# Layer 0's weight products with seven block products instead of eight, the last six batches' norm summed by TensorE, and another order of the preamble

## The chip, the core and the metric

The kernel runs on one NeuronCore of a Trainium2 chip: TensorE (matrix products, PE in the profile), VectorE (DVE), ScalarE (ACT), GpSimd (POOL), SyncE (SP, which here only issues DMAs), an SBUF and a PSUM of eight banks of 128 x 512 fp32. The metric is the device time of one execution in microseconds, the median of the runs. All arithmetic is fp32.

## The reference, cut to what matters

The input `x` is (64, 256, 128): 64 batches, 256 graph nodes, 128 channels. `adj` is 256 x 256. Four layers follow one another; each adds its result to its input and normalises over the channels.

```python
def ln(x): return (x - mean(x)) / sqrt(var(x) + 1e-5)          # over the 128 channels

# layer 0: powers of adj, seven weights (the second adjacency is the same adj)
x = ln(x + x@W0 + (A x)@(W1+W4) + (A A x)@(W2+W5) + (A A A x)@(W3+W6))
x = ln(x + A (x @ w) + bias)                                    # layer 1
x = ln(x + (D A^ D x) @ W.T + b)                                # layer 2
h = x                                                           # layer 3: 5 gated steps
for _ in range(5):
    m = A h                                                     # m_in = m_out
    z = sigmoid(m @ w3.T + h @ u3.T + b3);  r = sigmoid(m @ w4.T + h @ u3.T + b4)
    hv = tanh(m @ w5.T + (r * h) @ u5.T + b5)
    h = (1 - z) * h + z * hv
out = ln(x + h)
```

## The kernel before, in words

**Groups.** The 64 batches are worked in 32 groups of two batches (`NB = 2`), named by their first batch: 0, 2, ... 62. A group's tile is 128 partitions by 512 columns: 2 batches x 2 node halves (`T = 2`) x 128 channels. Up to ten groups are under way at once (`ACTIVE = 10`), in different layers, so that one group's products run while another waits for its elementwise work.

**Order.** Nothing is left to a run-time scheduler. `Plan` collects every operation with an engine, a cost, a lag and a rank, and `Plan.order` lays them out by a list schedule; each engine then executes its instructions strictly in that order. The buffers are slots by kind: `bank` (8, PSUM), `w` (64 tiles of 128 x 512), `th`, `q` and small ones for statistics. `Group.rank` sets which group goes first among ready operations. `pre` adds the operations of the preamble (weights, adjacency and constants), with a rank of their own; `fetch` and `load` are its DMAs, on the queue of SP or GpSimd. `Group.pe`, `dve` and `act` add a group's operations.

**A product.** `mm(o, lhsT, rhs, start, stop)` (L199) is one TensorE product, `lhsT` stationary (128 x 128), `rhs` moving (128, 256 or 512 wide). In the trace an fp32 product leaves two MATMUL records, a transpose through `ident` one.

**The adjacency products** (`propagate`, `seven`) already use seven block products instead of eight for a 2 x 2 block product, with sums ahead on GpSimd (L599, L603, L606) and sums behind on VectorE and ScalarE (L627 to L649).

**Layer 0.** With `q = A A x` it computes `s0 = x@W_0 + q@W_2 + A (x@W_1 + q@W_3)`, where the `W_k` in `w0s` are the summed weights, with the identity for the residual in `W_0` and each row's mean taken off, so that the result is centred. For each node half `t`, a bank `py0t` takes both products at once, 256 columns of weights wide:

```python
mm(o, (tiles if near else pairs)(xT)[:, b, t], w01.ap[:, 0:2, :], b == 0, True, shared=True)
mm(o, tiles(qT)[:, b, t], w0s.ap[:, 2:4, :], False, True, shared=True)
```

So a group has 2 halves x 2 batches x 2 = 8 products 256 wide. ScalarE copies the half that belongs under `A` to `v` (`moved`, L756), TensorE adds `A v` onto the other half (`second`, L764, 256 wide), ScalarE copies the sum to `s0` (`summed`, L768). The first two groups (`HEAD = 4` batches, `near`) get `xT` by TensorE transposes (L659). The other 30 get it by a VectorE transpose of 32 x 32 blocks (L730, `tx`), a store to DRAM (L733) and two loads (L738). For these the contraction rows come out permuted, and `w0p` is a copy of `w0s`'s first two weights with rows permuted alike (`permuted`, four DMAs, L308).

**Norms.** Layers 0 to 2 have centred sums: `spread_of` squares on ScalarE with an accumulated sum (L513), GpSimd takes the power -1/2 (L517, L518), ScalarE scales (L529). The last norm is not centred. It has `bn_stats` and `bn_aggr` on VectorE (L487, L491), the power on GpSimd (L498), and a scale and shift on ScalarE (L549).

**Layer 3** holds `hT`, the transposed state. Each step has five products 512 wide (`pr`, `ph`), two sigmoids and a tanh on ScalarE (L707), and `rh`, `d`, `e` and the new `hT` on VectorE (L714).

**The end.** After the last step the state must be turned back. Most groups do it by a VectorE transpose and DRAM (`tn`, `hn`). The last two groups (`END = 4` batches: 60 and 62) have TensorE transpose `hT` (L659, `pth`), VectorE add `y` (L541), take statistics and normalise too (L554).

**The preamble.** The first products need `ident` (GpSimd), the adjacency `a_nat`, its transpose `aT` and square `a2T`, the raw weights `w0_raw` of layer 0 and the first `x`. `warmed` issues 14 transposes that only keep TensorE busy (`WARM`). The small weights of layers 1 to 3 come by SP and GpSimd DMAs, are summed (`both`), centred (`wb`) and transposed (`transposed`, L397), all at ranks between 0.1 and 0.4.

Of the kernel before, what the change touches and what calls it, by code (L numbers as in the profile page):

```python
# [13 lines left out]
P = 128  # L14
# [5 lines left out]
END = 4  # L20
STEPS = 5
WARM = 14
# [135 lines left out]
def kernel(  # L158
# [42 lines left out]
    SHAPES = {"bank": [P, 512], "x": [P, 512], "w": [P, 512], "th": [P, 384], "q": [P, P], "st": [P, Q * 6], "mv": [P, Q * 2],  # L201
              "ve": [P, Q], "rs": [P, Q]}
    slots = {"bank": BANKS, "x": ACTIVE + 3, "w": 64, "th": 10, "q": 10, "dram1": 8, "dram2": 16, "st": 12, "mv": 12, "ve": 24, "rs": 12}
# [11 lines left out]
    def pre(rank, engine, cost, run, reads=(), writes=(), lag=None, joint=False):  # L215
        lag = lag or {"SP": 2300, "PE": 260, "DVE": 260, "ACT": 130, "POOL": 100}[engine]
        plan.add(engine, cost, lag, rank, run, reads, writes, joint=joint)
# [4 lines left out]
    def fetch(rank, o, src, v, queue):  # L222
        e, cost = QUEUES[queue]
        pre(rank, queue, cost, lambda: e.dma_start(o, src), [], [v], lag=3000, joint=True)
# [57 lines left out]
    w0_raw = load(0.01, "w0_raw", [P, C, K0], w0)  # L282
# [21 lines left out]
    w0p = constant("w0p", [P, 2, C])  # L304

    def permuted():
        for r in range(4):
            nc.sync.dma_start(w0p.ap.rearrange("(j r) k c -> r j k c", r=4)[r], w0s.ap[32 * r:32 * (r + 1), 0:2, :])  # L308

    pre(1.2, "SP", 1800, permuted, [w0s], [w0p])  # L310
# [61 lines left out]
    fetch(0.1, wb.ap[:, 0, :], w1, wb, "SP")  # L372
    for i, b in ((1, b1), (2, b2)):
        fetch(0.1, wb.ap[:, i, :], bass.AP(tensor=b.tensor, offset=b.offset, ap=[[0, P], [1, C]]), wb, "POOL")
    pre(0.35, "DVE", 1100, lambda: centre(wb, wbm), [wb], [wb, wbm])
    w1c, b1c, b2c = ((wb, wb.ap[:, i, :]) for i in range(3))
    raw = {name: load(0.1, f"raw_{name}", [P, src.shape[1]], src, False, "SP")
# [11 lines left out]
    def transposed(name, *parts_):  # L389
        ps, v = temp(f"p_{name}"), constant(name, [P, len(parts_) * P])  # L390

        def run():
            for i, src in enumerate(parts_):
                if src is raw["w2"]:
                    mm(ps.ap[:, i * P:(i + 1) * P], src.ap, less.ap, True, True)
                else:
                    nc.tensor.transpose(ps.ap[:, i * P:(i + 1) * P], src.ap, ident)  # L397

        n = len(parts_) * P
        pre(0.4, "PE", len(parts_) * 110, run, [*parts_, less], [ps])  # L400
        pre(0.4, "ACT", act_cost(n), lambda: nc.scalar.copy(v.ap, ps.ap[:, :n]), [ps], [v])
        return [(v, v.ap[:, i * P:(i + 1) * P]) for i in range(len(parts_))]
# [6 lines left out]
    for i, src in enumerate((w3_b, w4_b, w5_b, u3_b, u3_b, u5_b)):  # L409
        fetch(0.2, braw.ap[:, i:i + 1], src.rearrange("(p o) -> p o", o=1), braw, "POOL")  # L410
# [27 lines left out]
    class Group:  # L438
# [5 lines left out]

        def view(self, ap):
            return ap[self.start:self.start + self.nb].rearrange("b (t p) c -> p (b t) c", p=P)
# [11 lines left out]
        def add(self, engine, cost, lag, run, reads=(), writes=(), joint=False, behind=()):  # L458
            after = behind if self.first else self.gate
            self.count += 1  # L460
            op = plan.add(engine, cost, lag, self.rank(), run, reads, writes, after, joint)
            self.first = self.first or op
            self.last = op
            return op
# [15 lines left out]
        def statistics(self, tag, s, near):  # L480
            st, mv, ve, rs, nm = (self.val(k, n + tag) for k, n in (
                ("st", "st"), ("mv", "mv"), ("ve", "ve"), ("rs", "rs"), ("ve", "nm")))
            kept = () if near else (nm,)

            def stats():
                for q in range(self.q):
                    nc.vector.bn_stats(st.ap[:, q * 6:(q + 1) * 6], nat(s)[:, q, :])  # L487

            def aggr():
                for q in range(self.q):  # L490
                    nc.vector.bn_aggr(mv.ap[:, 2 * q:2 * q + 2], st.ap[:, q * 6:(q + 1) * 6])  # L491
                mean, var = (mv.ap.rearrange("p (q k) -> p k q", k=2)[:, k] for k in range(2))
                nc.vector.tensor_scalar(ve.ap, var, EPS, None, op0=OP.add)
                if not near:
                    nc.vector.tensor_scalar(nm.ap, mean, -1.0, None, op0=OP.mult)

            def scales():
                nc.gpsimd.tensor_tensor(rs.ap, ve.ap, half[:, :self.q], op=OP.pow)  # L498
                if not near:
                    nc.gpsimd.tensor_tensor(mv.ap[:, :self.q], nm.ap, rs.ap, op=OP.mult)  # L500

            self.dve(stats, [s], [st], 195 * self.q)
            self.dve(aggr, [st], [mv, ve, *kept], 67 * self.q + (142 if near else 240))
            self.add("POOL", 1010 if near else 1300, 100, scales, [ve, *kept], [rs] if near else [rs, mv])
            return mv, rs
# [33 lines left out]
        def residual(self, tag, ps, resid, left=lambda v: v.ap, right=lambda v: v.ap):  # L539
            s = self.val("w", "s" + tag)  # L540
            self.dve(lambda: nc.vector.tensor_add(right(s), left(ps), right(resid)), [ps, resid], [s])  # L541
            return (s, *self.statistics(tag, s, self.start >= B - END))

        def normalise(self, tag, s, mv, rs):
# [7 lines left out]
            def near():  # L552
                for q in range(self.q):
                    nc.vector.tensor_scalar(nat(y)[:, q, :], nat(s)[:, q, :], mv.ap[:, 2 * q:2 * q + 1],  # L554
                                            rs.ap[:, q:q + 1], op0=OP.subtract, op1=OP.mult)

            if self.start >= B - END:
                self.dve(near, [s, mv, rs], [y], 257 * self.q)
            else:
                self.act(run, [s, mv, rs], [y], 390 * self.q)  # L560
            return y
# [155 lines left out]
        def record(self):  # L717
# [5 lines left out]
            if near:  # L723
                xT, w01 = self.copied("xT", self.transposes("x", x_)), w0s
            else:

                w01 = w0p
                turn, far = self.val("w", "tx"), self.val("dram", "dx")
                xT = self.val("w", "xT")
                self.dve(lambda: nc.vector.transpose(  # L730
                    turn.ap.rearrange("p (r b i t) -> p r b t i", r=4, t=T, i=32),
                    x_.ap.rearrange("p (b t r j) -> p r b t j", r=4, t=T, j=32)), [x_], [turn])
# [9 lines left out]
            v, s0 = self.val("w", "v"), self.val("w", "s0")  # L742
            py = []

            for t in range(T):
                p = self.val("bank", f"py0{t}")
                py.append(p)

                def first(p=p, t=t):
                    for b in range(self.nb):  # L750
                        o = p.ap[:, b * 2 * C:(b + 1) * 2 * C]
                        mm(o, (tiles if near else pairs)(xT)[:, b, t], w01.ap[:, 0:2, :], b == 0, True, shared=True)
                        mm(o, tiles(qT)[:, b, t], w0s.ap[:, 2:4, :], False, True, shared=True)

                def moved(p=p, t=t):
                    nc.scalar.copy(parts(v)[:, t], four(p)[:, :, 1, :])  # L756

                self.pe(pe_cost(2 * C, 2 * self.nb), first, [xT, qT, w01, w0s], [p])
                self.act(moved, [p], [v], 55 + 107 * self.nb)
            for t in range(T):  # L760

                def second(p=py[t], t=t):
                    for kt in range(T):
                        mm(four(p)[:, :, 0, :], aT.ap[:, kt, t * P:(t + 1) * P], parts(v)[:, kt],  # L764
                           False, True, shared=True)

                def summed(p=py[t], t=t):
                    nc.scalar.copy(nat(s0).rearrange("p (b t) c -> p t b c", t=T)[:, t],  # L768
                                          four(p)[:, :, 0, :])

                self.pe(pe_cost(self.nb * C, T), second, [v, aT], [py[t]])
                self.act(summed, [py[t]], [s0], 55 + 107 * self.nb)
# [25 lines left out]
            for s in range(STEPS):  # L798
# [4 lines left out]
                r = self.gate_(f"r{s}", pr, AF.Sigmoid, rb)  # L803
                rh = self.tensor(f"rh{s}", OP.mult, r, hT)
# [7 lines left out]
                d = self.tensor(f"d{s}", OP.subtract, hv, hT)  # L812
                e = self.tensor(f"e{s}", OP.mult, z, d, into=pr)
# [8 lines left out]
            else:  # L822
                hT = self.tensor("hT", OP.add, hT, e, lambda v: v.ap.rearrange("p (k q i) -> p q k i", k=4, q=self.q),
                                 lambda v: v.ap.rearrange("p (q k i) -> p q k i", k=4, q=self.q))
                last = self.residual("3", self.transposes("h", hT), y)
# [68 lines left out]
```

## Time and profile before

| what | value |
|---|---|
| median of 3 runs | 1357.69 us (1357.1 to 1357.96) |
| the profiled execution | 1357.43 us |
| its span, first to last instruction | 1355.7 us |
| mean granted TensorE clock | 0.996 |
| TensorE busy, records of matmul | 1331.2 us, 6509 |
| VectorE / ScalarE / GpSimd busy | 953.2 / 756.0 / 678.0 us |
| first start of a TensorE record / last | 2.5 / 1345.8 us |
| layer 0's products, first and last start | 16.2 and 1080.9 us |

A row of the groups, for example `L199 PE MATMUL py<-v,aT 128*128 128x256 f32 x256`, names line, engine, operation, the tile written and the tiles read, the shape, and the number of records; a timeline row starts with its start in us and its length. A bracket at a row's end gives the engine's idle time ahead of it and what ended it. A matmul's length includes the drain of its pipeline, which overlaps the next one, so for TensorE the distance from start to start is the better price.

### The profile page before, as it was taken

Reading aid. Unit: us, or ns where it says so; the run is one execution under the profiler, and the core shown is the slowest. Engines: PE = TensorE matmul, PEld = TensorE weight load, DVE = VectorE, ACT = ScalarE, POOL = GpSimd, SP = SyncE. Lnnn points to the kernel's source line nnn. Section 1 sums busy time; section 2 is a strip of 40 time slices with the busy share of each in tenths; the row PEclk is TensorE's granted clock in tenths of the full one; section 3 lists DMA queues with packets and bytes.
Section 4 is the critical chain, followed back from the end, with each engine's and each line's share of the span. In section 5 each row is a group of like instructions: output and inputs, shape, how many; then the busy total and the mean of one; then the engine's idle time right before and its main releaser. Section 6 shows DMA issues by size and latency. Waiting matters only on the chain.

```text
span 1355.7 us, 21892 instructions
## 1 busy us (share of the span) xinstructions
PE 1331.2 (98%) x6509; PEld 922.0 (68%) x6509; DVE 953.2 (70%) x2343; ACT 756.0 (56%) x2398; POOL 678.0 (50%) x1095
## 2 busy tenths in 40 slices
PE   8999999999999999999999999999999999999995
PEld 7986666667676676776676667766776776566552
DVE  5366678778667677677767767776565778777778
ACT  4665464665456565657455466554655676444444
POOL 5786343654446544546364455543744685233322
PEclk9999999999999999999999999999999999999998
DMA  6322333434333322434243333332432233333333
GB/s 173 102 63 71 94 95 113 134 104 124 92 97 94 109 80 81 121 109 125 63 125 110 101 102 110 103 99 65 117 94 63 71 102 117 94 101 94 94 92 103
DMA packets 270214, 135.47 MB, mean 100 GB/s; under 512 B 175856, under 2 KB 241648, under 8 KB 270096
## 3 DMA queue, kind: packets, MB, share of 16 engines
q1 hardware_dynamic: 269840, 133.95, 34.1%
q8 instruction: 52, 0.85, 0.3%
q14 instruction: 66, 0.54, 0.1%
q0 software_dynamic: 256, 0.13, 0.1%
HBM read 67.57 MB, written 66.06 MB: 99 GB/s over the span
## 4 chain that ended last, share of the span: by engine, by line
PE 94%; DVE 3%; DMA 1%; issue 0%; ACT 0%; SPq 0%; POOL 0%; POOLq 0%; DVEq 0%; ACTq 0%
PE pr L199 30%; PE ph L199 20%; PE pmg L199 18%; PE py L199 15%; PE pm L199 7%; PE pmq L199 3%; DMA x<-in_x_dram 1%; DMA w_raw<-in_L_gnn_weight_dram 1%; DVE st L487 0%; DMA dx<-tx 0%; DVE s L541 0%; DVE rh L714 0%; DVE tx L730 0%; ACT y L529 0%; DVE y L554 0%
## 5 line engine op out<-in xcount | busy, mean ns | idle before, releaser
L199 PE MATMUL pr<-mg,w435u5T 128*128 128x512 f32 x640 | 320.3, 593 | 0.8 <-ACT r L707 0.8
L599 POOL TENSOR_TENSOR tsg<-h 128x256 f32<-128x256 f32 x128 | 96.4, 753 | 211.5 <-DMA h<-dh 145.0
L707 ACT ACTIVATE r<-pr,bsum 128x512 f32<-128x512 f32 x160 | 109.7, 686 | 151.1 <-PE pr L199 150.1
L714 DVE TENSOR_TENSOR rh<-r,hT 128x512 f32<-128x512 f32 x160 | 125.5, 787 | 71.6 <-ACT r L707 67.5
L707 ACT ACTIVATE pr<-pr,bsum 128x512 f32<-128x512 f32 x160 | 105.6, 660 | 120.7 <-PE pr L199 115.9
L199 PE MATMUL ph<-rh,w435u5T 128*128 128x512 f32 x320 | 164.1, 596 | 0.8 <-DVE rh L714 0.7
L714 DVE TENSOR_TENSOR d<-ph,hT 128x512 f32<-128x512 f32 x160 | 109.8, 686 | 78.3 <-ACT ph L707 77.3
L199 PE MATMUL ph<-mg,w435u5T 128*128 128x512 f32 x320 | 163.4, 593 | 0.0
L199 PE MATMUL pr<-hT,w2u3T 128*128 128x512 f32 x320 | 162.2, 592 | 0.0
L199 PEld LDWEIGHTS pr<-mg,w435u5T 128*128 128x128 f32 x640 | 109.0, 191 | 64.8 <-issue 48.6
L707 ACT ACTIVATE ph<-ph,bsum 128x512 f32<-128x512 f32 x160 | 105.5, 659 | 63.7 <-PE ph L199 62.9
L529 ACT ACTIVATE y<-s,rs 128x128 f32<-128x128 f32 x384 | 122.1, 392 | 15.4 <-POOL rs L518 14.7
L517 POOL TENSOR_SCALAR ve<-ve 128x4 f32<-128x4 f32 x96 | 22.6, 235 | 214.3 <-ACT y L513 214.2
L199 PEld LDWEIGHTS pmg<-s_aTp,tsg 128*128 128x128 f32 x768 | 102.1, 191 | 34.6 <-issue 30.7
L513 ACT ACTIVATE y<-s 128x128 f32<-128x128 f32 x384 | 113.7, 301 | 18.4 <-DVE s L536 18.2
L199 PEld LDWEIGHTS pmg<-aTp,h 128*128 128x128 f32 x512 | 88.0, 197 | 46.7 <-issue 35.1
L714 DVE TENSOR_TENSOR pr<-pr,d 128x512 f32<-128x512 f32 x160 | 110.6, 692 | 1.5
L627 DVE TENSOR_TENSOR usg<-usg,pmg 128x128 f32<-128x128 f32 x160 | 45.2, 284 | 91.9 <-PE pmg L199 67.2
L714 DVE TENSOR_TENSOR hT<-hT,pr 128x512 f32<-128x512 f32 x160 | 108.6, 680 | 1.7
L199 PE MATMUL pmg<-s_aTp,tsg 128*128 128x128 f32 x768 | 106.4, 275 | 0.0
L518 POOL TENSOR_TENSOR rs<-ve,half 128x4 f32<-128x4 f32 x96 | 99.6, 1038 | 8.0
L637 DVE TENSOR_TENSOR mg<-pmg,usg 128x256 f32<-128x256 f32 x160 | 67.1, 420 | 51.7 <-PE pmg L199 49.9
(175 smaller groups left out, 2805.5 us busy)
## 6 DMA issues: line engine op xcount, KB each, us to landing
dh<-th SPq DMA_DIRECT2D x160, 256.0 KB, 2.1
h<-dh SPq DMA_DIRECT2D x256, 128.0 KB, 2.5
x<-in_x_dram SPq DMA_DIRECT2D x32, 256.0 KB, 3.2
hT<-dh SPq DMA_DIRECT2D x128, 64.0 KB, 2.0
out_dram<-y SPq DMA_DIRECT2D x32, 256.0 KB, 2.3
dx<-tx SPq DMA_DIRECT2D x30, 256.0 KB, 2.7
xT<-dx SPq DMA_DIRECT2D x60, 128.0 KB, 2.6
dn<-tn SPq DMA_DIRECT2D x30, 256.0 KB, 2.0
```

The source lines that it names most:

```text
L199: nc.tensor.matmul(o, lhsT, rhs, start=start, stop=stop, skip_group_check=shared)
L513: nc.scalar.activation(nat(y)[:, q, :], nat(s)[:, q, :], AF.Square, scale=C ** -0.5, accum_out=ve.ap[:, q:q + 1])
L517: nc.gpsimd.tensor_scalar(ve.ap, ve.ap, EPS, None, op0=OP.add)
L518: nc.gpsimd.tensor_tensor(rs.ap, ve.ap, half[:, :self.q], op=OP.pow)
L529: nc.scalar.mul(nat(y)[:, q, :], nat(s)[:, q, :], rs.ap[:, q:q + 1])
L599: nc.gpsimd.tensor_tensor(ts.ap[:, :2 * P].rearrange("p (x c) -> p x c", x=2), ins(h)[:, 1], ins(h)[:, :, 0], op=OP.subtract)
L627: nc.vector.tensor_tensor(row(u, 0), row(u, 1), row(ps, 3), op=OP.add)
L637: nc.vector.tensor_tensor(o(m, slice(1, 3)), o(ps, slice(1, 3), False), both, op=OP.add)
L707: self.act(lambda: nc.scalar.activation(t.ap, ps.ap, func, bias=bias[1], scale=1.0), [ps, bias[0]], [t], act_cost(self.width) + 100)
L714: self.dve(lambda: nc.vector.tensor_tensor(out(t), way(a), way(b), op=op), [a, b], [t])
```

## The change

1. **Layer 0, groups 4 to 62** (`inner_seven`). The products of (x, q) for two node halves with the four weights are a 2 x 2 block product with eight blocks; it is now formed with seven. VectorE forms four sums per group (`sd`, `ss`, `se`, `sf`, 128 x 256, in a new kind of buffer `h`), TensorE makes 7 products 128 wide for each of two batches into two banks (`py0`, `pz0`), VectorE adds the pieces (`u2`, `u3`, both halves of `v`, one half of `s0`), ScalarE copies `u1` and the other half of `s0`. The weight sums are made once (`w0_blocks`, `w0t`). Groups 0 and 2 keep the old form, now `inner`.
2. **The input transpose** of these groups reads `x` in steps of four columns, so that the contraction rows come out in natural order. `w0p` and its four DMAs are gone. Its cost in the plan is 1000 instead of 640.
3. **The last norm of groups 58, 60 and 62** (`END = 6`, `closing`). TensorE sums `y`, `hT` and `e` into one bank `s3`, multiplying `hT` and `e` with `less` (the identity less 1/128) so that the sum comes out turned and centred (`y` is centred already). The norm is then `spread_of` and one VectorE product. ScalarE copies `hT` in the order of tiles (`hc`).
4. **The preamble.** `w0_raw` has rank -1 instead of 0.01, so its load stands ahead of the second `x`. `WARM` is 12. GpSimd's weight loads stand behind `ident` (`made`), the six bias loads behind those. The small weights' loads, sums and transposes have later ranks.
5. **Buffers**: 48 `w` slots instead of 64, and 14 `h` slots of half that size.

The core of the diff:

```diff
-END = 4
+END = 6
-WARM = 14
+WARM = 12
-    slots = {"bank": BANKS, "x": ACTIVE + 3, "w": 64, "th": 10, ...
+    slots = {"bank": BANKS, "x": ACTIVE + 3, "w": 48, "th": 10, "q": 10, "h": 14, ...
...
-    w0_raw = load(0.01, "w0_raw", [P, C, K0], w0)
+    w0_raw = load(-1, "w0_raw", [P, C, K0], w0)
...
-    pre(1.2, "SP", 1800, permuted, [w0s], [w0p])
+    w0t = constant("w0t", [P, 4, C])
+    def w0_blocks():
+        nc.vector.tensor_sub(t1, w_1, w_0)
+        nc.vector.tensor_sub(t2, w_3, t1)
+        nc.vector.tensor_sub(t3, w_3, w_1)
+        nc.vector.tensor_sub(t4, w_2, t2)
+    pre(1.2, "DVE", 1000, w0_blocks, [w0s], [w0t])
...
-    fetch(0.1, wb.ap[:, 0, :], w1, wb, "SP")
+    made = pre(-9, "DVE", 100, lambda: nc.vector.tensor_copy(wb.ap[:, 1:3, 0], ident[:, :2]), [], [wb])
+    fetch(0.6, wb.ap[:, 0, :], w1, wb, "SP")
...
-    pre(0.35, "DVE", 1100, lambda: centre(wb, wbm), [wb], [wb, wbm])
+    pre(0.9, "DVE", 1100, lambda: centre(wb, wbm), [wb, w0s], [wb, wbm])
-    raw = {name: load(0.1, ...
+    raw = {name: load(0.6, ...
...
-        pre(0.4, "PE", len(parts_) * 110, run, [*parts_, less], [ps])
-        pre(0.4, "ACT", act_cost(n), lambda: nc.scalar.copy(v.ap, ps.ap[:, :n]), [ps], [v])
+        pre(2.1, "PE", len(parts_) * 110, run, [*parts_, less], [ps])
+        pre(2.1, "ACT", act_cost(n), lambda: nc.scalar.copy(v.ap, ps.ap[:, :n]), [ps], [v])
...
+        def inner_seven(self, xT, qT):
...
+            self.add("DVE", 340, 260, s3, [xT], [sd])
+            self.add("DVE", 340, 260, s1, [xT, qT], [ss])
+            self.add("DVE", 340, 260, s2, [xT, ss], [st_])
+            self.add("DVE", 340, 260, s4, [qT, st_], [sf])
...
+            self.pe(pe_cost(P, NB), lambda: times(half(out_, 0), at(xT, 0), w0s.ap[:, 0, :], True), [xT, w0s], [out_])
+            self.act(lambda: nc.scalar.copy(u1.ap, out_.ap[:, :N]), [out_], [u1], 270)
+            self.pe(pe_cost(P, 2 * NB), both, [ss, st_, w0t], [more])
+            self.pe(pe_cost(P, NB), lambda: times(half(out_, 0), at(qT, 0), w0s.ap[:, 2, :]), [qT, w0s], [out_])
+            self.pe(pe_cost(P, NB), lambda: times(half(out_, 1), at(qT, 1), w0t.ap[:, 3, :]), [qT, w0t], [out_])
+            add(lambda: (u2.ap, u1.ap, more.ap[:, :N]), [u1, more], [u2])
+            self.pe(pe_cost(P, NB), lambda: times(half(more, 0), whole(sd), w0t.ap[:, 2, :]), [sd, w0t], [more])
+            add(lambda: (u3.ap, u1.ap, more.ap[:, :N]), [u1, more], [u3])
+            add(lambda: (half(v, 1), whole(u3), half(more, 1)), [u3, more], [v])
+            self.pe(pe_cost(P, NB), lambda: times(half(more, 1), whole(sf), w0s.ap[:, 3, :]), [sf, w0s], [more])
+            add(lambda: (half(v, 0), whole(u2), half(more, 1)), [u2, more], [v], True)
...
+        def closing(self, y, hT, e, behind):
+            s, hc = self.val("bank", "s3"), self.val("w", "hc")
+            self.act(lambda: nc.scalar.copy(out_(hc), way(hT)), [hT], [hc])
...
+            def early():
+                turned(hc, True, False)
+                mm(s.ap, ident, y.ap, False, False, shared=True)
+            self.pe(pe_cost(P, self.q) + pe_cost(self.width), early, [hc, y, less], [s], behind=(behind,))
+            self.pe(pe_cost(P, self.q), lambda: turned(e, False, True), [e, less], [s])
+            o, rs = self.spread_of("3", s)
...
-                    x_.ap.rearrange("p (b t r j) -> p r b t j", r=4, t=T, j=32)), [x_], [turn])
+                    x_.ap.rearrange("p (b t j r) -> p r b t j", r=4, t=T, j=32)), [x_], [turn], 1000)
...
+                if s == STEPS - 1 and self.start >= B - END:
+                    e = self.tensor("e", OP.mult, z, d, *self.by_tile)
+                    break
...
-                hT = self.tensor("hT", OP.add, hT, e, ...
-                last = self.residual("3", self.transposes("h", hT), y)
+                o = self.closing(y, hT, e, gated)
```

`behind=(behind,)` makes the early part of `closing` wait in the plan for the last step's `r`.

## The prediction

> **What bounds the kernel now.** I read the busy shares first, then the slices:
>
> ```profile
> span 1355.7 us, 21892 instructions
> PE 1331.2 (98%) x6509; PEld 922.0 (68%) x6509; DVE 953.2 (70%) x2343; ACT 756.0 (56%) x2398; POOL 678.0 (50%) x1095
> PE   8999999999999999999999999999999999999995
> PEclk9999999999999999999999999999999999999998
> PE 94%; DVE 3%; DMA 1%; issue 0%; ACT 0%; SPq 0%; POOL 0%; POOLq 0%; DVEq 0%; ACTq 0%
> ```
>
> TensorE works in every slice but the last at full clock, and is 94% of the chain that ended last. Ends of matmuls are modelled, so I checked starts instead. TensorE's timeline in mid-kernel:
>
> ```profile
> 600.12 1.02 PE L199 MATMUL ph<-mg,w435u5T 128*128 128x512 f32 x2
> 602.97 1.06 PE L199 MATMUL py<-wb,m 128*128 128x128 f32 x8
> 603.86 1.02 PE L199 MATMUL pr<-mg,w435u5T 128*128 128x512 f32 x2
> 605.81 1.03 PE L199 MATMUL py<-v,aT 128*128 128x256 f32 x4
> 606.67 0.39 PE L199 MATMUL pmg<-s_aTp,h 128*128 128x128 f32 x2
> ```
>
> Eight records 128 wide start within 603.86 - 602.97 = 0.89 us, four records 256 wide within 0.86. Over the whole trace the median distance between starts is 112, 216 and 429 ns for widths 128, 256 and 512. Each fp32 product leaves two records, so a product costs 0.224, 0.432 and 0.858 us. All records at these distances make 1318.6 us; from the first start (2.5 us) to the last (1345.8) only some 25 us are anything else. Between 70 and 1330 us it is 9 us. So TensorE time is kernel time, but for two places. One is the head (7 us lost up to 50 us). The other is the end, by the timelines of TensorE, ScalarE, VectorE and GpSimd, in that order:
>
> ```profile
> 1336.14 1.12 PE L199 MATMUL pr<-mg,w435u5T 128*128 128x512 f32 x2 [0.78 <-ACT r L707]
> 1337.49 1.13 PE L199 MATMUL ph<-rh,w435u5T 128*128 128x512 f32 x2 [0.23 <-DVE rh L714]
> 1345.12 1.12 PE L659 MATMUL pth<-ident,hT 128*128 128x128 f32 x4 [5.64 <-DVE hT L714]
> ...
> 1340.17 0.63 ACT L707 ACTIVATE ph<-ph,bsum 128x512 f32<-128x512 f32 x1
> ...
> 1342.12 0.67 DVE L714 TENSOR_TENSOR d<-ph,hT 128x512 f32<-128x512 f32 x1
> 1347.34 0.69 DVE L541 TENSOR_TENSOR s<-pth,y 128x512 f32<-128x512 f32 x1
> 1350.53 1.12 DVE L554 TENSOR_SCALAR y<-s,mv,rs 128x128 f32<-128x128 f32 x4 [1.12 <-POOL rs L498]
> ...
> 1349.49 1.01 POOL L498 TENSOR_TENSOR rs<-ve,half 128x4 f32<-128x4 f32 x1 [0.77 <-DVE ve L493]
> ```
>
> The last large product ends at 1338.6; the last result is ready at 1351.65, 13.0 us later, with VectorE in order and nearly full. Store and finish take 4.05 more.
>
> **What the Trainium skill says.** "TensorE: Matmul & The Clock Gate", section "Wait — 56ns, not 53.3ns?", gives N/2.4 + about 2.5 ns from start to start, 55.6 at N = 128. Twice that is our 112: the trace agrees, and splitting a wide product costs the fixed part again. "VectorE: DVE Perf Modes", section on the errata, gives (N+151)/0.96 ns for an fp32 addition: 424 at 256; the 128x256 additions here show 420, and start 335 to 340 ns apart. "SBUF — State Buffer", section "Who interferes with whom", says that a VectorE operation with two SBUF inputs and a GpSimd one that reads SBUF block each other. Here L714's `rh` (two SBUF inputs) means 787 ns, its `hT` (one in PSUM) 680. The same page, section on the DMA port swizzle, has 16-byte lines, with a penalty for each access that goes to a new one. The new input transpose reads with a step of 4 fp32, which no row of this trace shows.
>
> **Part 1: layer 0, 30 of 32 groups.** Before, 8 products 256 wide: 8 x 0.432 = 3.456 us. After, 14 of 128: 14 x 0.224 = 3.136. That is one eighth less arithmetic, partly paid back in fixed parts: 0.32 us a group, **9.6 us** in 30. The adjacency products (`py<-v,aT`, 256 wide) stay. All of it is TensorE time where TensorE is full.
>
> VectorE gets nine 128x256 operations per group (four sums ahead, five behind), 9 x 0.335 = 3.0 us. With the stepped read I take 1.0 us instead of 0.63 for the transpose (bounds 0.63 and 2). In 30 groups that is about 100 us: 70% busy becomes 78%, still below TensorE. ScalarE loses two of four copies (L756, L768, 370 ns): 22 us less. What hides the handoffs is other groups' work: in the built program's order, at least 1.1 us of other products stand between a group's last block product and its adjacency product, with a median of 3.7. The handoff needs the product's end after its last start (275 - 112 ns, 0.16) and one addition (0.42), 0.6 in all. Behind `u1`'s copy, TensorE's second product into the same half is at least 0.86 us away. Where VectorE is late, these products stand at the head of TensorE's queue, and everything behind them waits. TensorE's 9 us of mid-kernel loss came at 70%; in proportion to busy/(1 - busy), 2.3 to 3.5, it would be 14 if VectorE caused all of it. The list of waits names VectorE or ScalarE as TensorE's releaser for some 2 us of them. I take **+2 us** (bounds 0 and 8). Fewer `w` buffers (48 for 64) cost nothing: at most 28 are live at once in the order. The 14 small `h` buffers (two groups' worth) are all in use, but only space the groups. A layer-0 bank opens earlier and stays longer, the bank of `pmq` shorter; summed over all, 5.3 banks are open on average instead of 5.2.
>
> **Part 2: the last norm.** Per closing group TensorE gets 4 products of `hc`, one 512 wide of `y`, 4 of `e`: 8 x 0.224 + 0.858 = 2.65 us, three times, for 4 transposes (0.45) twice. Ahead of the last large product stand group 58's both parts and group 60's first, 1.75 + 0.9 + 1.75 = 4.4 us. Group 60's first part lies where TensorE now waits 0.78 + 0.23, so **+3.4 us**. After the last large product: ScalarE's `hv` 0.8, `d` 0.7, `e` 0.6. TensorE meanwhile does 0.9 + 1.75 of closing, which ends about 0.5 later, then 0.9 for `e`. Then a wait for ScalarE (0.35, behind group 56's `y`), squares 1.2, GpSimd 0.1 + 1.3 (L517, L518), the product 0.7: **7.2 us** for 13.0. The chain no longer holds `hT`, four statistics, the aggregate and four normalisations on VectorE, nor other groups' statistics between them. Gain 5.8, net **2.4** (bounds -1 and 5; a throttled clock would double the last 0.9). The next late thing is ScalarE's queue: squares of 60 and `y` of 56 ahead of 62's squares.
>
> **Part 3: the head.** GpSimd now finishes `ident` (2.46 us) ahead of its first DMA issue (0.77), two warm-up records go (0.23 each, cold), and L308's four issues (2.4 us of SP's queue) go. The weights of layer 0, 7.1 us under way to 9.4, are issued one load earlier. Against it, `p_an` stands ahead of group 2's transposes and waits for VectorE's `ahat`, which follows those weights: TensorE idles there for 1 to 2 us, and group 2's `x` lands later. The 1.2 us wait for `raw_u` goes, since those transposes stand behind layer 0's first products. On VectorE the small weights' centring moves behind, so the first input transpose starts about 1.5 us earlier, and with it the dependent `x` loads on SP. Taken **-1.3 us** (bounds -3 and +2).
>
> **Sum**: -9.6 + 2 - 2.4 - 1.3 = -11.3. The profiled execution took 1357.43 (span 1355.7 and 1.7 around it), 0.26 below the median of the runs; that gives **1346 us**.
>
> **Rivals.**
> (a) VectorE eats the gain in part: at 8 us mid-kernel instead of 2 the time is 1352. For it: in the busiest slices VectorE is at 8 tenths already. Against: between 70 and 1330 TensorE idles visibly 2 us.
> (b) Slower: the longer layer-0 chain stops TensorE. Place: `v` from VectorE ahead of `py<-v,aT`, with TensorE's in-order queue behind it. Without the +2, the sum is -13.3, so break-even is 13.3 / 30 = 0.44 us a group. One exposed handoff of 0.6 in each makes 18 - 13.3 = +4.7, 1362. It needs VectorE to run later than its order by over a microsecond in most groups, as with an input transpose of 2 us or more. Nothing in the trace shows such backlog.
> (c) The tail doesn't shrink because ScalarE and GpSimd queue there: net +1 instead of -2.4, 1349.5.
> That the seven-product form is not used is excluded: the built order has 14 products for these groups.
>
> **Chances**: forecast 0.66 (own range 1341 to 1351), (a) 0.14, (b) 0.12, (c) 0.08. The range reaches over (a) and (c), 1340 to 1355. 0.2% is 2.7 us, about what a measurement of this kernel can tell from no change; of (a) a part falls within it. Faster 0.82, same 0.06, slower 0.12.
>
> **What would show it.** Right: TensorE busy some 11 us less; `py`/`pz` rows at 112 ns starts; VectorE near 1050 us; last result about 7 us after the last large product; the input transpose's mean near 1 us. Wrong: idle before `py<-v` or `pz` released by VectorE, summing to over 5 us; or ScalarE's `y` rows late in the last 10 us.

## The result and the profile after: no change, 1357.5 us

The changed kernel takes 1357.54 us (median of 4 runs, 1355.93 to 1359.89); the kernel before takes 1357.39 beside it (1356.96 to 1357.96). The ratio is 1.0002, 95% interval 0.9985 to 1.002. The forecast was 1346, its range 1340 to 1355. So the saved arithmetic brought nothing. The page of the changed kernel: busy shares, TensorE's slices and clock, and the chain that ended last.

```profile
span 1355.6 us, 23005 instructions
...
PE 1335.0 (98%) x6913; PEld 932.5 (69%) x6913; DVE 1057.5 (78%) x2578; ACT 740.7 (55%) x2361; POOL 687.8 (51%) x1097
...
PE   8999999999999999999999999999999999999998
...
PEclk9999999999999999999999999999999999999999
...
PE 92%; DVE 5%; ACT 1%; DMA 1%; issue 1%; SPq 0%; POOLq 0%; DVEq 0%; ACTq 0%; POOL 0%
```

The span is the old one within 0.1 us. The last slice of TensorE is full (8 for 5), so the tail did shrink. VectorE's busy time is up 104 us, and its share of the last chain rose from 3% to 5%. TensorE's busy time even rose by 3.8 us: it is the time in which at least one record is under way, up to its modelled end. It gained 9.6 us in the last 26 us of the span, where TensorE used to wait, and lost 6.0 us in mid-kernel, so it is no measure of work here.

So I count starts, as the prediction did. Each record is priced at 112, 216 or 429 ns by its width; what the distance to the next start exceeds that by is **loss**. The span then splits into parts (us; "last large product" is the last `ph<-rh`):

| | before | after | difference |
|---|---|---|---|
| first start of TensorE | 2.5 | 1.4 | -1.2 |
| loss in the head, up to 70 us | 7.3 | 9.6 | +2.3 |
| work up to the last large product | 1317.7 | 1312.3 | -5.4 |
| loss from 70 to 1330 us | 9.3 | 22.0 | **+12.7** |
| loss from 1330 us on | 1.6 | 0.0 | -1.6 |
| from the last large product to the end of the span | 17.2 | 10.3 | -6.9 |
| span | 1355.7 | 1355.6 | -0.1 |

Everything that was to be saved is there. It is taken back by one row, the loss in mid-kernel. A view that shows it without my sum is busy time by stretch. These rows, of the kernel before and of the changed one, are for 70 to 1330 us; after the length of the stretch come the busy times of PE, PEld, DVE, ACT and POOL, then the granted clock, the DMA share and GB/s.

```profile
70.00:1330.00 1260.00, 1257.76 (x6096) 860.08 (x6094) 900.13 (x2175) 706.45 (x2216) 626.08 (x1010) 1.00 0.34 98
```

```profile
70.00:1330.00 1260.00, 1251.74 (x6395) 861.22 (x6394) 987.96 (x2388) 690.63 (x2159) 633.67 (x1009) 1.00 0.33 97
```

Visible idle of TensorE is 1260 less the first number: 2.2 us before, 8.3 after. (A 128-wide record's modelled length is 275 ns where the next one can start after 112, so a gap of under some 0.16 us doesn't show. This idle is therefore smaller than the loss by starts, but it ranks the kernels in nearly the same way.) The clock is 1.00 in both.

**Who waits?** I expected layer 0's own products, `py<-v` and `pz`. TensorE's groups of the changed kernel, with the idle time ahead of them in the last column:

```profile
L199 PE MATMUL py<-v,aT 128*128 128x256 f32 x256 | 65.3, 380 | 0.3 <-DVE v L640 0.3
...
L199 PE MATMUL pz<-w0t,se 128*128 128x128 f32 x120 | 18.5, 277 | 0.4 <-DVE d L836 0.4
...
L199 PE MATMUL pz<-w0s,sf 128*128 128x128 f32 x120 | 18.2, 277 | 0.7 <-DVE v L640 0.7
```

With 0.1 us ahead of `py<-w0s,xT` that is 1.5 us in all. By starts, 2.7 of the 22.0 us of loss stand directly ahead of layer 0's products (0.4 of 9.3 before). The list of TensorE's waits between 70 and 1330 us has other groups' products on top; its columns are us in total, times, longest:

```profile
PE pmg L199 <- DVE mg L755: 1.3, 2, 0.7
PE pr L199 <- DVE mg L759: 1.3, 2, 1.0
PE pm L199 <- DVE hT L836: 0.7, 1, 0.7
PE pz L199 <- DVE v L640: 0.7, 2, 0.4
```

So layer 0's new form slows down work that it doesn't touch. There are two things by which it could: VectorE's time, and PSUM banks. The trace, read with the listed order of the products, gives how long layer 0's banks are open in each group, from the first to the last product into them. Before, 31.5 us on average of the 32 groups (two banks, 15.7 each in the mean). After, 64.2 us: in the 30 groups of the new form a `pz` bank is open for 15 us on average, but a `py` bank for 53. The timeline of TensorE in the changed kernel shows one such group:

```profile
590.82 0.63 PE L199 MATMUL py<-w0s,xT 128*128 128x128 f32 x4
...
619.05 0.61 PE L199 MATMUL pz<-w0t,se 128*128 128x128 f32 x4
...
624.09 0.61 PE L199 MATMUL py<-w0s,mq 128*128 128x128 f32 x4
...
660.24 1.03 PE L199 MATMUL py<-v,aT 128*128 128x256 f32 x4
```

The first product needs `xT` alone and is placed as soon as that is there. It opens the bank at 590.8; the next product into this bank comes 33 us later, when `qT` is ready. For these 33 us the bank holds one finished piece. This is one of the longest waits: over the 30 groups it is 16.0 us on average (1.3 to 35). In the old form a product could only open its bank when `xT` and `qT` were both there.

### The profile page after: what moved, and what is told of

Same layout as the page of the kernel before. It is cut to its first block, busy times and chain, and to the rows that moved or that the text cites. A ratio compares the mean times of both kernels' runs of the same rounds, so it can differ in the third digit from the quotient of the medians.

```text
span 1355.6 us, 23005 instructions
## 1 busy us (share of the span) xinstructions
PE 1335.0 (98%) x6913; PEld 932.5 (69%) x6913; DVE 1057.5 (78%) x2578; ACT 740.7 (55%) x2361; POOL 687.8 (51%) x1097
## 4 chain that ended last, share of the span: by engine, by line
PE 92%; DVE 5%; ACT 1%; DMA 1%; issue 1%; SPq 0%; POOLq 0%; DVEq 0%; ACTq 0%; POOL 0%
PE pr L199 30%; PE ph L199 20%; PE pmg L199 18%; PE py L199 10%; PE pm L199 7%; PE pz L199 3%; PE pmq L199 3%; DMA w_raw<-in_L_gnn_weight_dram 1%; PE s L199 0%; DVE rh L836 0%; DVE pr L836 0%; DVE hT L836 0%; DVE d L836 0%; DMA x<-in_x_dram 0%; ACT y L519 0%
## 5 line engine op out<-in xcount | busy, mean ns | idle before, releaser
L519 ACT ACTIVATE y<-s 128x128 f32<-128x128 f32 x396 | 117.0, 299 | 29.0 <-DVE s L542 22.5
L524 POOL TENSOR_TENSOR rs<-ve,half 128x4 f32<-128x4 f32 x99 | 103.5, 1046 | 8.2
```

Of the source, the lines that this page charges most:

```text
L519: nc.scalar.activation(nat(y)[:, q, :], nat(s)[:, q, :], AF.Square, scale=C ** -0.5, accum_out=ve.ap[:, q:q + 1])
```

## The experiments

Theories. **V**: VectorE's additional time delays the operands of other groups. **B**: layer 0's banks, open twice as long, leave fewer banks for the other groups, and the order that the planner can then list runs with less slack. **L**: the list of the change is merely an unlucky one. The experiments' chips gave 1358.5 to 1358.7 us for the kernel before; ratios are to runs of it on the same chip. All of them in one table; "loss" is that from 70 to 1330 us, "layer-0 banks" the open time a group (us, mean of 32), and VectorE's busy time is that of the same stretch. "Idle in the plan" comes from no trace: `Plan.order` gives every operation a start and a cost when the kernel is built, and this is the time for which TensorE then has nothing to do, between 70 and 1300 us of the plan's own clock.

| kernel | median | ratio, 95% interval | loss | idle in the plan | layer-0 banks | VectorE |
|---|---|---|---|---|---|---|
| before | 1357.4 | 1 | 9.3 | 6.9 | 31.5 | 900 |
| the change | 1357.5 | 1.0002 [0.9985, 1.0020] | 22.0 | 22.9 | 64.2 | 988 |
| vector_load | 1370.1 | 1.0085 [1.0068, 1.0102] | 21.9 | 7.9 | 36.6 | 984 |
| load_few_columns | 1359.1 | 1.0003 [0.9995, 1.0012] | 10.3 | 7.9 | 36.2 | 932 |
| seven_banks | 1371.5 | 1.0092 [1.0077, 1.0107] | 23.1 | 23.9 | 33.8 | 891 |
| hold_bank | 1376.4 | 1.0128 [1.0113, 1.0143] | 27.3 | 28.9 | held by a read | 880 |
| few_columns | 1353.5 | 0.9959 [0.9945, 0.9973] | 19.5 | 22.9 | 64.0 | 936 |
| late_open | 1351.0 | 0.9941 [0.9926, 0.9956] | 13.7 | 9.2 | 49.9 | 991 |
| late_few_columns | 1346.4 | 0.9910 [0.9896, 0.9925] | 10.3 | 9.2 | 49.6 | 938 |
| order_nudged | 1362.8 | 1.0033 [1.0022, 1.0045] | 25.7 | 28.0 | 66.9 | 980 |
| late_nudged | 1351.2 | 0.9948 [0.9934, 0.9963] | 14.2 | 11.6 | 56.7 | 992 |
| late_opened_early | 1370.5 | 1.0088 [1.0073, 1.0103] | 26.7 | 27.1 | 73.6 | 973 |
| late_twice | 1360.6 | 1.0013 [1.0007, 1.0020] | 17.0 | 15.7 | 57.8 | 977 |
| layer0_alone | 1365.9 | 1.0054 [1.0039, 1.0069] | 27.1 | 26.3 | 65.4 | 983 |
| closing_alone | 1355.1 | 0.9975 [0.9966, 0.9984] | 9.2 | 6.9 | as before | 899 |
| head_alone | 1358.4 | 0.9996 [0.9988, 1.0005] | 8.5 | 6.0 | as before | 895 |
| late_two_closing | 1353.6 | 0.9964 [0.9951, 0.9977] | 15.3 | 9.5 | 50.0 | 990 |

### Each suspect put into the kernel before: vector_load, seven_banks, hold_bank

vector_load, behind `qT` in the 30 groups:

```diff
+            if not near:
+                va = self.val("w", "va")
+                for k in range(9):
+                    self.dve(lambda k=k: nc.vector.tensor_tensor(va.ap[:, :N], (qT if k % 3 else xT).ap[:, :N], xT.ap[:, N:],
+                                                                 op=OP.add), [qT, xT], [va], 340)
```

> The kernel before, and in each of the 30 later groups nine more VectorE additions of 128x256 (on xT and the q product, their result unused), known to the plan: VectorE's load of the change without its products, banks or chain. If VectorE's load is what makes TensorE wait (70% to 78% busy), TensorE loses 20 us or more between 70 and 1330 us instead of 9, and the time rises by 8 to 13 us, to 1366 to 1371. If PSUM banks are the cause, TensorE's loss stays at 7 to 13 us and the time within 4 us of 1357.5.

seven_banks:

```diff
-BANKS = 8
+BANKS = 7
```

> The kernel before with 7 PSUM banks in the plan instead of 8. It prices a bank. If banks are scarce already, TensorE's loss between 70 and 1330 us rises by 10 us or more (time 1367 to 1375); if there are banks to spare, so that holding layer 0's banks longer can't matter, it stays within 3 us of 1357.5.

hold_bank lets VectorE read four columns of one of layer 0's banks once layer 1's `m` is there, which keeps that bank from being used again until then:

```diff
+            held = py[:1]
...
+                if tag == "1" and not near:
+                    for p in held:
+                        scrap = self.val("ve", "scrap")
+                        self.dve(lambda p=p, scrap=scrap: nc.vector.tensor_copy(scrap.ap, p.ap[:, :4]), [p, m], [scrap], 140)
```

> The kernel before, and in the 30 later groups one of layer 0's two PSUM banks is read once more, four columns by VectorE, after layer 1's adjacency product is done: the bank stays occupied some 20 us longer per group, VectorE has 0.1 us more. If banks are the cause, TensorE's loss between 70 and 1330 us rises from 9 to 20 to 30 us and the time by 10 to 20 us. If VectorE's load is the cause, the time stays within 2 us of 1357.5.

All three cost 11 to 18 us on the kernel before, all of it in mid-kernel. Busy time from 70 to 1330 us of hold_bank:

```profile
70.00:1330.00 1260.00, 1247.80 (x6020) 854.73 (x6020) 880.45 (x2145) 696.37 (x2204) 623.34 (x1004) 1.00 0.33 96
```

TensorE's visible idle is 12.2 us for 2.2, with VectorE busy 20 us less than before (fewer operations fall in the stretch, as the kernel is longer). So a bank held longer is enough by itself. VectorE's time is also enough by itself, by vector_load. These runs show that both can cost as much as was lost; they don't tell which did in the change.

### The same order with less VectorE time: few_columns, load_few_columns

few_columns is the changed kernel with layer 0's sums made for one column in 128 and the old step of the input transpose; load_few_columns is vector_load with two columns in its additions. One line of each:

```diff
-                nc.vector.tensor_tensor(whole(sd), at(xT, 0), at(xT, 1), op=OP.subtract)
+                nc.vector.tensor_tensor(few(whole(sd)), few(at(xT, 0)), few(at(xT, 1)), op=OP.subtract)
```

```diff
-    nc.vector.tensor_tensor(va.ap[:, :N], (qT if k % 3 else xT).ap[:, :N], xT.ap[:, N:], ...
+    nc.vector.tensor_tensor(va.ap[:, :2], (qT if k % 3 else xT).ap[:, :2], xT.ap[:, N:N + 2], ...
```

> The changed kernel with its listed order, waits, banks and products kept instruction for instruction, but eight of the nine VectorE additions of layer 0 work on one column per batch instead of 128 (the products then read that column over and over), and the input transpose reads x as before; so layer 0's numbers are wrong, and VectorE has some 75 us less to do. If VectorE's load makes TensorE wait, TensorE's loss between 70 and 1330 us falls from 22 to 9 to 14 us and the time to 1344 to 1350. If it is held banks or the listed order as such, the loss stays at 18 to 22 us and the time at 1353 to 1358.

> The kernel of vector_load with its listed order kept, but the nine added operations work on 2 columns instead of 256: the order is that of vector_load, VectorE's load nearly that of before. If VectorE's time itself cost the 11 us of vector_load, the time falls back to 1357 to 1361; if the other order of the list did it, it stays at 1366 to 1371.

load_few_columns gives back nearly all (loss 10.3), so in vector_load it was indeed the time. few_columns does not. Its row of busy times from 70 to 1330 us:

```profile
70.00:1330.00 1260.00, 1253.16 (x6394) 861.78 (x6394) 936.47 (x2396) 690.39 (x2158) 624.33 (x1007) 1.00 0.34 98
```

With 52 us less VectorE time in the stretch the loss goes from 22.0 to 19.5 only, and the head's from 9.6 to 8.5. The time is 4 us less by the medians, 6 by the ratios (two chips). In the change, **V** holds for a small part. (Why the same amount of VectorE time costs so much more in vector_load was not tested. There the nine additions stand one behind the other, and all nine, not four of nine, read two SBUF inputs; the last section shows what that costs.)

### The bank opened later: late_open

One word: the first product is also made to wait, in the plan, for `qT`. The products, the additions and their number are the same. The mean wait for the second product into that bank falls from 16.0 to 6.9 us.

```diff
-            self.pe(pe_cost(P, NB), lambda: times(half(out_, 0), at(xT, 0), w0s.ap[:, 0, :], True), [xT, w0s], [out_])
+            self.pe(pe_cost(P, NB), lambda: times(half(out_, 0), at(xT, 0), w0s.ap[:, 0, :], True), [xT, qT, w0s], [out_])
```

> The changed kernel, where layer 0's first block product (x by the first weight) also waits in the plan for the q product, so that its bank is opened later; all operations and VectorE's load are those of the changed kernel. From first to last product layer 0's banks are open 50 us per group instead of 63 (32 before). If banks are the cause, TensorE's loss between 70 and 1330 us falls from 22 to 10 to 17 us and the time to 1345 to 1352. If VectorE's load is the cause, 20 to 24 us and 1355 to 1360. If it is only the luck of the listed order, anything between.

```profile
70.00:1330.00 1260.00, 1256.10 (x6434) 866.28 (x6434) 990.67 (x2410) 694.74 (x2172) 635.05 (x1013) 1.00 0.34 98
```

That is its row of busy times by stretch: TensorE idles 3.9 us for 8.3, while VectorE is as busy as in the change (990.67 and 987.96). The time is 1351.0, ratio 0.9941: faster than both kernels, than the changed one by 6.5 us by the medians and 8 by the ratios.

### Both taken away: late_few_columns

> late_open's order with few_columns' VectorE additions: both the banks' time and about 75 us of VectorE time are taken away. As in few_columns, the sums of layer 0 ahead and behind are made for one column in 128 and that column is read for all, and the input transpose reads as before the change. If the two causes add up: few_columns gained 4 on the change, so 1347, mid-kernel loss 10 to 11. If VectorE's time only costs where banks are short: 1350 to 1351, mid-kernel loss 13 to 14. If VectorE's time were the larger cause: 1344 or less.

Its row of busy times from 70 to 1330 us:

```profile
70.00:1330.00 1260.00, 1257.82 (x6443) 867.61 (x6442) 937.97 (x2421) 695.83 (x2170) 626.03 (x1013) 1.00 0.34 98
```

The time is 1346.4 us, the loss 10.3. Of the 12.7 us that the change had added, 1.0 is left. The two causes add up. By this route banks are 22.0 - 13.7 = 8.3 and VectorE 13.7 - 10.3 = 3.4; by the other (few_columns first) VectorE 22.0 - 19.5 = 2.5 and banks 19.5 - 10.3 = 9.2. (The change's buffers, 48 `w` and 14 `h`, were not tested alone. This kernel has them too, so they can't hold much of the loss.)

### Is it the luck of the list? order_nudged, late_nudged

In both, one number of the plan; the instructions stay, their order changes.

```diff
-            return self.add("DVE", cost or dve_cost(self.width), 260, run, reads, writes, joint)
+            return self.add("DVE", cost or dve_cost(self.width), 265, run, reads, writes, joint)
```

> The changed kernel with the planner's lag of one kind of VectorE operation at 265 instead of 260: the same instructions, listed in another order. It tells how much of a time is the luck of one order. Layer 0's banks are open 66 us a group in it (63 in the change). If held banks set the time: 1357 to 1360. If the change's list was merely unlucky: several us less, 1348 to 1354, with mid-kernel loss near 14.

> late_open with the same lag of 265. Layer 0's banks are open 56 us a group (late_open 50, the change 63). Held banks: mid-kernel loss between late_open's 13.7 and the change's 22.0, by proportion 18, so about 1355. Luck of the list: no relation to order_nudged, anywhere from 1349 to 1360, and as likely above order_nudged as below it.

late_nudged is late_open again, within 0.2 us by the medians and 1 us by the ratios; order_nudged is some 4 us slower than the changed kernel by the ratios. Neither came out at the time that its expectation gave for held banks: about 1355 for the one, 1357 to 1360 for the other. So the luck of a list is worth some us. The one other list of the change is worse, so nothing speaks for an unlucky one, and both lists with the late bank beat both with the early one by 6 us or more.

### Bank or place: late_opened_early, late_twice

late_open also moves a product, so the pair below keeps everything else. Both add one product per group, which the proper one overwrites; they differ in one input that it waits for.

```diff
+            self.pe(pe_cost(P, 1), lambda: mm(half(out_, 0)[:, 0], at(xT, 0)[:, 0], w0s.ap[:, 0, :], True, True, shared=True), [xT, w0s], [out_])
```

> late_open with one product more per group: the first block product (x with W_0, for one batch) is made once as early as in the change, which only opens layer 0's first bank, and again at late_open's place, where it overwrites the first. The addition is 0.224 us x 30 = 6.7 us of TensorE in itself. By the listed order layer 0's banks are open 72 us a group. If a bank held open is the cause: mid-kernel loss 22 or more, about 1366 to 1372. If the place of the other products in the list is what late_open gained from: loss near 14, about 1358.

In late_twice its inputs are `[xT, qT, w0s]`.

> The control of late_opened_early: the same product is made twice, both times at late_open's place, so that the bank stays closed until then (57 us a group). The same 6.7 us of TensorE. Held banks: mid-kernel loss 14 to 16, about 1358. Place in the list alone: the same as late_opened_early.

Busy time by stretch, late_opened_early first, then late_twice:

```profile
70.00:1330.00 1260.00, 1248.93 (x6415) 863.46 (x6415) 973.21 (x2362) 687.54 (x2156) 631.92 (x1006) 1.00 0.33 96
```

```profile
70.00:1330.00 1260.00, 1254.34 (x6454) 868.36 (x6453) 977.10 (x2385) 690.76 (x2170) 627.62 (x1008) 1.00 0.33 97
```

TensorE idles 11.1 us in the one and 5.7 in the other; the loss by starts is 26.7 and 17.0, the times 1370.5 and 1360.6 (about 1358 and a loss of 14 to 16 were expected of late_twice). Ten us hang on when a bank is opened, more than twice what the nudged lists moved. **B** is shown. Sorted by layer 0's mean number of open banks (open time x 32 groups / 1350 us), four kernels with all the additional VectorE work stand in one row: 1.18 banks, loss 13.7 (late_open); 1.37, 17.0 (late_twice); 1.52, 22.0 (the change); 1.75, 26.7 (late_opened_early). The others fit less exactly: late_nudged has 1.34 and 14.2, layer0_alone 1.55 and 27.1, order_nudged 1.59 and 25.7.

How a missing bank turns into late operands can be read from the plan. An operation that opens a bank gets no start before a bank is free. seven_banks differs from the kernel before in nothing but the number of banks, and TensorE's idle time in its plan is 23.9 us for 6.9. Only 7.0 of this is TensorE itself waiting for a bank. In 15.9 us it waits for an operand from ScalarE or VectorE, whose own work now comes later (5.9 before). In the change it is 6.1 us of 22.9 and 14.7. So most of the loss in mid-kernel was in the list before the kernel ran: but for vector_load, the idle time in the plan follows the measured loss within 6 us in every row of the table. It doesn't show what vector_load's additions cost on the chip (7.9 for 21.9), so it can't divide the change's loss between the two causes.

### The parts alone: layer0_alone, closing_alone, head_alone

Each is the kernel before with one part of the change's diff and nothing else: `inner_seven` with its transpose and buffers; `closing` with `END = 6`; the preamble.

> The kernel before with the seven block products of layer 0, the stepped transpose and the buffers of the change, but the last norm and the preamble of before. By the forecast's part 1 it is 9.6 - 2 us faster, 1350. By the theory that VectorE's load and held banks raise TensorE's loss between 70 and 1330 us by 13 us, it is 3 us slower than before, 1359 to 1363.

> The kernel before with only the last norm of groups 58, 60 and 62 changed. By the forecast's part 2, TensorE's last large product ends 3.4 us later and the result is ready 7.2 us behind it instead of 13.0: 2.4 us faster, 1354 to 1356. If the tail only moves the wait to ScalarE and GpSimd, 1358 to 1360.

> The kernel before with the preamble of the change and nothing else. By the prediction's part 3 it gains 1.3 us: about 1357.2 where the kernel before takes 1358.5. By the profile of the change (head loss 9.6 us for 7.3, first start 1.2 us earlier) it loses about 1.2: 1359.7, with p_an waiting 2 to 3 us for ahat. If the head's loss in the change came from layer 0's new VectorE work behind it, it is within 0.5 of the kernel before.

Layer 0 alone costs 7.5 us, the closing gains 3.4, the head is within the noise. (`permuted` goes with layer 0, so head_alone still has its four DMAs.) Layer 0's cost is larger than the expected 3 us: its loss is 27.1, not 22.0. Their sum, +4.0, is not the +0.2 of the whole. The whole's interval reaches from -2.0 to +2.7 us, and each part makes another list. The ends of the plans do the same: +7.6, -4.6 and +0.1 us for the three parts, -0.3 for the whole (1333.1 for 1333.4).

### A smaller closing: late_two_closing

late_open with `END = 4`.

> late_open with the last norm summed by TensorE for groups 60 and 62 only (END = 4); group 58 goes by VectorE's transpose and DRAM as before. The prediction prices a closing group at 2.65 us of TensorE, and nothing in the tail depends on group 58: 1351 - 2.65, about 1348.5. If group 58's residual on VectorE then stands in the tail's way: 1351 to 1353.

1353.6, slower than late_open by 2 to 3 us. Group 58's norm then stands in the tail, as the rival in the expectation said, and the mid-kernel loss is 1.6 us higher. ScalarE's last row of group 58's norm:

```profile
1347.36 1.65 ACT L555 ACTIVATE y<-s,mv,rs 128x128 f32<-128x128 f32 x4 [2.73 <-POOL mv L506]
```

It ends at 1349.0 as the last computing instruction, 9.3 us after the last large product ended (late_open: 6.9). late_open, at 1351.0 us, remains the version to use; few_columns and late_few_columns leave out most of layer 0's sums and are no versions of the kernel.

## Why the prediction was wrong, and where it was right

**Layer 0's products: right.** They start 112 ns apart (above: `pz<-w0t,se`, four records, at 619.05; the four of `pz<-w0t,ss` at 619.50). The work up to the last large product fell by 5.4 us: 9.6 less for layer 0, 4.4 more for closing, the rest in the preamble.

**The elementwise prices: right in sum, too low for the sums ahead.** VectorE's groups of the changed kernel:

```profile
L850 DVE STREAM_TRANSPOSE tx<-x 128x512 f32<-128x512 f32 x30 | 33.1, 1107 | 4.5 <-DMA x<-in_x_dram 4.5
...
L612 DVE TENSOR_TENSOR sd<-xT 128x256 f32<-128x256 f32 x30 | 16.8, 559 | 1.7 <-DMA xT<-dx 1.7
...
L640 DVE TENSOR_TENSOR v<-u,pz 128x256 f32<-128x256 f32 x60 | 24.5, 411 | 4.7 <-PE pz L199 4.3
```

The stepped transpose takes 1.1 us for the 1.0 that was taken. The four sums ahead take 466 to 559 ns on average; where the next operation follows at once, it starts 390 to 500 ns later, for the 335 that was taken. VectorE is busy 1057 us for the "near 1050".

**The mid-kernel term: the step that failed.** "I take +2 us (bounds 0 and 8)" was +12.7. The 2 us were VectorE's, and for VectorE alone they were about right: 2.5 to 3.4 us. The rest is the banks', and for them the prediction took nothing. It wrote "A layer-0 bank opens earlier and stays longer", but read "summed over all, 5.3 banks are open on average instead of 5.2" as *nothing changes*. That term is 8 to 9 us.

By the traces the sum did stay: 5.0 before, 5.2 after, counted from first to last product. But layer 0's part of it went from 0.75 to 1.52, and the other kinds gave up 0.6 of a bank: `pmq` 0.97 to 0.66, `pm` 0.83 to 0.67, `pmg` 1.12 to 1.05. That the others are pushed out, and not merely changed, is seen in seven_banks, where the products are those of before and `pmq` and `pm` shrink alike, to 0.65 and 0.66. A mean of 5 of 8 also looks roomier than it is: a bank is free only when its readers are done with it. Counted so, in the plan, 6.7 are held on average before and 6.9 after, and all eight for 29% and 38% of the time.

The cover that the prediction looked at instead, "at least 1.1 us of other products stand between", was a look at layer 0's own handoffs, and these nearly held (1.5 us of idle, 2.7 us by starts). The plan from which it was read already had TensorE idle for 22.9 us for 6.9, and its end at 1333.1 us for 1333.4: no gain.

**The closing: right.** The timelines of TensorE, ScalarE, GpSimd and VectorE at the end:

```profile
1344.39 1.02 PE L199 MATMUL ph<-rh,w435u5T 128*128 128x512 f32 x2
...
1347.89 1.05 PE L199 MATMUL s<-less,e 128*128 128x128 f32 x8
...
1349.05 0.28 ACT L519 ACTIVATE y<-s 128x128 f32<-128x128 f32 x1
...
1350.58 1.04 POOL L524 TENSOR_TENSOR rs<-ve,half 128x4 f32<-128x4 f32 x1
...
1351.65 0.69 DVE L681 TENSOR_TENSOR y<-s,rs 128x512 f32<-128x512 f32 x1 [2.01 <-POOL rs L524]
```

The last large product ends at 1345.4 and the last result is ready at 1352.3, 6.9 us later; 7.2 was forecast, 13.0 it was. The wait for ScalarE behind group 56's `y` was taken at 0.35 us and is 0.1: the products of `e` end at 1348.94, the squares start at 1349.05. closing_alone gives -3.4 us [-4.6, -2.2] for the forecast -2.4.

**The head: not confirmed, within its bounds.** The forecast was -1.3. In the trace of the change TensorE starts 1.2 us earlier but loses 2.3 more; head_alone measures -0.5 [-1.6, +0.7], which excludes neither nothing nor the forecast. What was too low is the 1 to 2 us for `p_an`. TensorE's and VectorE's rows in the changed kernel:

```profile
10.24 0.83 PE L259 MATMUL p_an<-ident,ahat 128*128 128x128 f32 x4 [2.51 <-DVE ahat L338]
...
9.84 0.61 DVE L338 TENSOR_SCALAR ahat<-ahat,dinv 128x256 f32<-128x256 f32 x2
```

`ahat` stands in VectorE's queue behind the sums of `w0s`, which wait for `w_raw` until 8.66. TensorE idles there for 2.5 us (3.7 in head_alone). Behind it the granted clock was 0.5 from 10.9 to 14.3 us; the sixteen 256-wide records from 11.7 to 16.5 us took 4.75 us for the 3.46 of their price. The trace of before has no such stretch there, that of closing_alone has one, so it isn't shown to come from the change. The head also forecast the first input transpose 1.5 us earlier; it came at 22.0 for 21.2. The centring of `wb`, which was to move behind it, still stands ahead (19.8 to 21.1), and the sums of `w0t` (21.1 to 22.0) are new.

**Its own marks.** "TensorE busy some 11 us less" did not follow from its parts: layer 0 is -9.6, but three closing groups add 8.0 and two groups' transposes take off 0.9, so all records together had to be about 3 less, as they are by starts (1318.6 to 1315.8). The mark "idle before `py<-v` or `pz` summing to over 5 us" stayed silent while 12.7 us were lost: it watched the changed instructions only. Rival (b) needed these handoffs to be exposed and fell. Rival (a) had the right kind of loss, at 8 us for 12.7, but named VectorE, the smaller cause.

## What to carry to other kernels

In a kernel whose order comes from a plan with few buffers, price a change also in buffer time, bank x us per group, and not only in engine time: here an early product that opens a bank and then waits 16 us on average for its partner cost about 8 us, nearly what the seven products saved, and making it wait for its partner's input gained 6 to 8 us. Where the mean occupancy stays level while one user doubles, ask whether the others were pushed out. If the plan keeps times, read its end and its idle time before anything is run: they held most of this result. And look for the loss at the neighbours: the operations that a change touches can all be on time while those of other groups are late.

## What the runs showed of the hardware that was not expected

- VectorE's 128x256 fp32 sums with two SBUF inputs took 466 to 559 ns on average in the change, the same addition with one input in PSUM 411. The trace shows where the difference comes from (GpSimd's spans in it are rough). Of the 120 sums, the 78 that start while a GpSimd instruction is under way mean 564 ns, up to 1392; the other 42 mean 412, and none is over 427. In few_columns, with 2 elements a partition, the two kinds mean 328 and 152 ns, so the delay of some 150 to 180 ns hardly depends on the size. The additions with a PSUM input show no such difference (403 to 412 ns either way). That agrees with the Trainium skill, "SBUF — State Buffer", section "Who interferes with whom", which has a VectorE instruction with two SBUF inputs contend with a GpSimd instruction that reads SBUF.
- A 128x512 stream transpose that reads with a step of four fp32 takes 1107 ns instead of 703; in few_columns, which reads as before, it is 702 again.
- One PSUM bank less of eight cost 12.8 us (0.9%) in a kernel whose mean was 5.0 open banks, counted from first to last product.
